# Scores of the segmented attention on 64 partitions a head, with the rotary exchange done by transfers inside the chip

## The chip, the cores and the metric

The kernel runs on one core of one Trainium2 chip. Its engines are TensorE (PE, with its weight loads shown apart as PEld), VectorE (DVE), ScalarE (ACT), GpSimd (POOL) and SyncE (SP, which here issues nearly all DMAs). The metric is the device time of one execution in microseconds (us). All arithmetic on the matrices is in float32.

## What is computed

Sixteen sequences of 256 tokens with 256 features pass through two layers, each adding to the residual x: a cross attention and a causal attention of 16 heads of 16 features; a feed-forward block with blockwise 4-bit rounding; a diffusion step followed by a segmented attention; and a mixture of eight experts. The change lies in the segmented attention, of 16 heads with 64 features. Cut to its core, the reference says:

```python
def _rotate_half(t):
    t2 = t.reshape(*t.shape[:-1], t.shape[-1] // 2, 2)
    return jnp.stack((-t2[..., 1], t2[..., 0]), axis=-1).reshape(t.shape)
x = seq * jax.lax.rsqrt(jnp.mean(seq * seq, axis=-1, keepdims=True) + eps) * g_norm
q, k, v = jnp.split(x @ W_qkv, 3, axis=-1)
q = q * cos + _rotate_half(q) * sin
k = k * cos + _rotate_half(k) * sin
...
k = jnp.concatenate((pmk, k), axis=-2)
v = jnp.concatenate((pmv, v), axis=-2)
scores = jnp.einsum('bhid,bhjd->bhij', q, k) * dh ** (-0.5)
scores = jnp.where(mask, scores, NEG_INF)
attn = jax.nn.softmax(scores, axis=-1)
out = jnp.einsum('bhij,bhjd->bhid', attn, v)
```

Segments have 128 tokens, so a sequence has two; each segment sees 16 learnt keys and values (pm) ahead of its own. The rotation pairs an even with an odd feature: the new even one is even x cos - odd x sin, the new odd one is odd x cos + even x sin.

## The kernel before

The program has two parts. `woven` (L292) runs everything up to the second residual, and `mixture` (L1034) the experts. Only the first is touched.

In `woven` nine generators, the stages, each yield one operation at a time: `stage_a` and `stage_e` the first two attentions, `stage_gate`, `stage_up` and `stage_down` the rounding of the feed-forward weights at the start, `stage_f` the feed-forward block, `stage_p` the diffusion and the projections of the segmented attention, `stage_g` its scores, `stage_v` its values. `weave` (L182) is a planner: it knows a cost for each operation (`Unit.cost`, L164), 4.5 us for the landing of a DMA issued by SP (`LANDING`) and 0.15 us for a hop between engines; it keeps for each tile when it was last written and read, takes the operation of all stages that could start first, issues it and goes on. So the order of each engine's queue is fixed when the program is built, and each engine executes it in that order. In the profile all woven operations have the same line, L160, where `Unit` makes the call; they are told apart by tiles.

The segmented attention works on groups of four heads; a sequence has four groups, the whole run 64. For each group, `project4` (L897) loads four pieces of weights (wq in two parts, wv, wo), multiplies them with the normalised input zT, and rotates query and key. The weights of a group are laid out by the host so that the 128 rows of the first half of the product are the 32 even features of four heads and those of the second half the 32 odd ones:

```python
yield g.pool.tensor_tensor(dst[0], by_seg(t1[:, 0, :]), by_seg(t2[:, 1, :]), ALU.subtract)
yield g.pool.tensor_tensor(dst[1], by_seg(t1[:, 1, :]), by_seg(t2[:, 0, :]), ALU.add)
```

Even and odd features of a head thus stand on the same partitions, one behind the other in the free dimension; t1 and t2 (f_t in the profile) are DVE's products with cosine and sine, read from PSUM, and POOL adds them into f_q or into `keys[n]`. `keys[n]` holds, for each half and segment, the 16 learnt keys ahead of 128 keys of the sequence.

`scores4` (L955) takes two heads at a time. For each segment it multiplies the even and then the odd features of each head, both on 32 partitions, and adds them up in PSUM: 2 segments x 2 halves x 2 heads = 8 matmuls of 32 partitions x 144 columns. DVE adds the causal mask and takes the maximum, ACT exponentiates, POOL scales. `values4` (L988) transposes the probabilities and multiplies by values and output weights. A group is admitted to `project4` when the values of the group three before it have been planned.

PSUM is held in two pairs of banks and four single banks, which stages take and give back. SBUF buffers are rings by name: t1 and t2 have one each, wq and wv two, f_q and wo three. `stage_p` begins when the first batch of the first attention and the three weight roundings are planned. `project_heads` (L467) does the rotation of the first attention with two products in b_t1 and b_t2 and a sum on POOL. `fetch_a` (L413) loads the inputs of a batch, xT with two buffers. In `stage_f` each batch also issues two DMAs of 1 MB that fill ysort with zeros.

Of the kernel before, what the change touches and what calls it, by code (L numbers as in the profile page):

```python
# [19 lines left out]
P = 128  # L20
# [42 lines left out]
def setup(ctx, tc, a, n_batch):  # L63
# [29 lines left out]
    nc.gpsimd.memset(k.zero, 0.0)  # L93

# [87 lines left out]
def weave(streams):  # L182
# [8 lines left out]
    def ready(op, engine):  # L191
# [4 lines left out]
        for x in op.outs:  # L196
            n = x.tensor.name
            before = [written.get(n), read.get(n)]
            ring = rings.get(getattr(x.tensor, "tag", None), [])
            if n not in ring and ring:  # L200
                bufs = x.tensor.bufs or x.tensor.tag_meta.bufs
                if len(ring) >= bufs:
                    before += [written.get(ring[-bufs]), read.get(ring[-bufs])]
            for p in before:
                if p:
                    t = max(t, p[0] + (HOP if p[1] != engine else 0.0))
# [85 lines left out]
def woven(k):  # L292
    nc, tc = k.nc, k.tc
    with ExitStack() as ctx:
# [13 lines left out]
        g.x, g.io, g.done = {}, {}, {"W": 0, "A": 0, "M": 0, "E": 0, "F": 0, "P": 0, "G": 0, "V": 0, "L": 0}  # L308
        with tc.manual_schedule():
            weave([stage_a(g), stage_e(g), stage_gate(g), stage_up(g), stage_down(g), stage_f(g), stage_p(g), stage_g(g), stage_v(g)])  # L310
# [102 lines left out]
def fetch_a(g, b):  # L413
# [3 lines left out]
    xT = g.a_.tile([P, 2, S], F32, name="xT", tag="xT", bufs=2)  # L417
# [49 lines left out]
def project_heads(g, hT):  # L467
# [8 lines left out]
    for st in range(2):  # L476
# [320 lines left out]

def stage_p(g):
    k, a = g.k, g.a
    yield lambda: g.done["A"] > 0 and g.done["W"] == 3  # L800
# [38 lines left out]
    g.keys = []  # L839
    for n in range(4):  # L840
        pmk = tile_l(g, [P, 2, 4 * PM], "pmk", 2)
        yield g.sp.dma_start(out=pmk, in_=a["pmk"][:, n])
        t = g.w.tile([P, 2, 2, PM + P], F32, name=f"keys{n}")
        for j in range(4):
            rows = row32(j, 32)
            src = pmk[rows, :, j * PM : (j + 1) * PM]
            yield g.pool.tensor_copy(t[rows, :, :, 0:PM], src.unsqueeze(2).to_broadcast([32, 2, 2, PM]))
        g.keys.append(t)
    g.mhalf = g.w.tile([P, 2], F32, name="mhalf")
# [47 lines left out]
def project4(g, n, zT):  # L897

    a = g.a
# [8 lines left out]
    by_seg = lambda t: t.rearrange("p (s t) -> p s t", s=2)  # L908
    for which in range(2):
# [4 lines left out]
        t1, t2 = tile_l(g, [P, 2, S], "f_t1"), tile_l(g, [P, 2, S], "f_t2")  # L914
# [13 lines left out]
    g.singles.append(one)  # L928
    return q, v, wo
# [25 lines left out]
def scores4(g, n, q, v, wo):  # L955
# [554 lines left out]
```

## Time and profile before

| what | value |
|---|---|
| median of 3 runs | 2941.87 us (2941.02 to 2943.33) |
| profiled execution, its own time | 2943.53 us |
| its span in the profile | 2941.8 us |
| mean granted TensorE clock | 0.963 |
| PE, PEld busy in the span | 2768.7, 2072.5 us |
| DVE, ACT, POOL busy | 1428.6, 924.0, 842.2 us |
| DMA moved | 265.66 MB, mean 90 GB/s |
| woven part | up to about 1897 us |

A group of the profile gives line, engine, operation, the tiles written and read, the shape and the count, then busy time in us and mean duration in ns, then the engine's idle time just before these instructions and what ended it. Records of PE overlap, so the busy time of a group divided by its count is its pace and is shorter than the mean duration of one. For a matmul the shape is given as rows x columns of the array used, then partitions x streamed columns. A row of the waits gives the waiting engine and tile, what ended the wait, the total in us, how often, and the longest. A stretch gives its length, then the busy us of PE, PEld, DVE, ACT and POOL with their instruction counts, the granted clock, the share of the DMA engines and GB/s.

### The profile page before, as it was taken

The numbers are of one execution on the slowest core, as the hardware profiler recorded it, in microseconds if no ns is written. First come the engines' busy times: TensorE is split into PE (matmuls) and PEld (weight loads), VectorE is DVE, ScalarE is ACT, GpSimd is POOL, SyncE is SP. The second block draws the span as 40 slices with busy tenths as digits, with TensorE's granted clock in tenths as the row PEclk, the third lists the DMA queues.
The fourth block names the chain that finished last, engine by engine and source line by source line (L and its number), as shares of the span: only waits on it lengthen the run. The fifth ranks groups of instructions, "written<-read, shape, count | busy, mean of one in ns | idle before, by whom it ended". The sixth has DMA issues, their size and how long they took to land. (4 is left out here: it accounts for less than half of the span.)

```text
span 2941.8 us, 42036 instructions
## 1 busy us (share of the span) xinstructions
PE 2768.7 (94%) x15979; PEld 2072.5 (70%) x15979; DVE 1428.6 (49%) x3073; ACT 924.0 (31%) x2416; POOL 842.2 (29%) x1023
## 2 busy tenths in 40 slices
PE   5899999999999999999999989689999999999999
PEld 3666667777777777767777767545566888888865
DVE  6566666676676676675776655413240000000023
ACT  2223333333333333423334333223321222222221
POOL 4333333433344343343343333202220000000034
PEclk7799999999899999999999999889999999999999
DMA  3122122122122132222221222231111355555523
GB/s 107 55 93 73 53 92 84 56 80 74 59 91 69 58 97 69 63 92 69 64 92 35 76 90 74 87 93 51 51 38 67 108 179 179 179 181 179 177 85 95
DMA packets 191230, 265.66 MB, mean 90 GB/s; under 512 B 34217, under 2 KB 161970, under 8 KB 181682
## 3 DMA queue, kind: packets, MB, share of 16 engines
q1 hardware_dynamic: 184882, 246.16, 26.2%
q0 software_dynamic: 6144, 16.79, 1.8%
q8 instruction: 128, 2.10, 0.3%
q14 instruction: 76, 0.62, 0.1%
HBM read 202.34 MB, written 60.56 MB: 89 GB/s over the span
## 5 line engine op out<-in xcount | busy, mean ns | idle before, releaser
L160 ACT ACTIVATE f_prob<-pair,f_stat 128x144 f32<-128x144 f32 x512 | 190.7, 377 | 270.2 <-DVE f_stat L160 258.8
L160 DVE TENSOR_TENSOR pair<-pair,mask 128x256 f32<-128x256 f32 (+1 forms) x384 | 197.8, 516 | 123.1 <-PE pair L160 83.2
L49 PE MATMUL bank<-ysT,w 128*128 128x256 f32 x1120 | 249.3, 381 | 5.7 <-ACT ysT L113 5.7
L160 PE MATMUL single<-e_zT,wq 128*128 128x256 f32 x1024 | 254.1, 392 | 0.0
L1155 POOL DMA_INDIRECT got<-osort,pos_o x64 | 62.3, 973 | 662.8 <-ACT hT L1103 608.5
L49 PE MATMUL bank<-w,ehT 128*128 128x256 f32 x1120 | 247.4, 379 | 0.0
L49 PEld LDWEIGHTS bank<-ysT,w 128*128 128x128 f32 x1120 | 211.3, 190 | 38.0 <-ACT ysT L113 9.9
L49 PEld LDWEIGHTS bank<-w,ehT 128*128 128x128 f32 x1120 | 212.8, 190 | 28.9
L160 PEld LDWEIGHTS single<-e_zT,wq 128*128 128x128 f32 x1024 | 193.4, 196 | 32.9 <-issue 2.7
L1140 ACT ACTIVATE ehT<-bank,own_b 128x256 f32<-128x256 f32 x280 | 132.5, 473 | 241.6 <-PE bank L49 241.6
L160 POOL TENSOR_SCALAR_AFFINE_SELECT b_e<-b_e 128x512 f32<-128x512 f32 x128 | 86.5, 676 | 329.9 <-ACT b_e L160 329.9
L160 PE MATMUL pair<-keys,f_q 32*128 32x144 f32 x2048 | 164.9, 300 | 0.9 <-ACT b_e L160 0.7
L160 PEld LDWEIGHTS pair<-keys,f_q 32*128 32x128 f32 x2048 | 137.2, 190 | 35.9 <-issue 28.6
L160 ACT ACTIVATE b_e<-pair 128x768 f32<-128x768 f32 x128 | 103.6, 810 | 166.4 <-PE pair L160 153.3
L160 PE MATMUL single<-wo,f_oT 128*128 128x256 f32 x512 | 129.8, 386 | 9.5 <-ACT f_oT L160 8.4
L160 POOL TENSOR_TENSOR f_q<-f_t,f_t 128x256 f32<-128x256 f32 x128 | 91.6, 734 | 160.9 <-DVE f_t L160 151.4
L160 PE MATMUL pair<-b_qkT 16*128 16x128 f32 (+1 forms) x1024 | 127.3, 373 | 11.0 <-ACT b_qkT L160 8.0
L1145 DVE COPY eo<-bank 128x512 f32<-128x512 f32 x35 | 24.2, 692 | 230.9 <-PE bank L49 230.9
L160 DVE TENSOR_REDUCE qpad<-pair 128x2 f32<-128x256 f32 (+1 forms) x256 | 131.0, 554 | 4.4
L1259 POOL DMA_INDIRECT ysort<-r_y,r_posi x64 | 62.6, 978 | 241.0 <-DMA ysort<-r_y,r_posi 97.0
L160 DVE TENSOR_TENSOR x<-x,single 128x512 f32<-128x512 f32 (+1 forms) x112 | 68.0, 607 | 128.7 <-PE single L160 128.1
L160 POOL TENSOR_TENSOR keys<-f_t,f_t 128x256 f32<-128x256 f32 x128 | 95.2, 762 | 118.8 <-DVE f_t L160 117.6
(295 smaller groups left out, 5319.7 us busy)
## 6 DMA issues: line engine op xcount, KB each, us to landing
w<-in_w SPq DMA_DIRECT2D x70, 1024.0 KB
ysort<-zero SPq DMA_DIRECT2D x32, 1024.0 KB
wq<-in_w_qk SPq DMA_DIRECT2D x128, 256.0 KB
wv<-in_w_v SPq DMA_DIRECT2D x64, 256.0 KB
wo<-in_w_out SPq DMA_DIRECT2D x64, 256.0 KB
ys<-ysort SPq DMA_DIRECT2D x35, 256.0 KB
osort<-eo SPq DMA_DIRECT2D x35, 256.0 KB
xT<-in_xT SPq DMA_DIRECT2D x16, 256.0 KB
```

Of the source, the lines that this page charges most:

```text
L49: nc.tensor.matmul(out, lhsT, rhs, start=start and i == 0, stop=stop and i == last)
L160: return Op([(self.name, self.cost(fn, outs, aps), lambda: call(*args, **kw))], outs, aps)
L1140: nc.scalar.activation(hT[:, f, :], ph, AF.Gelu_apprx_tanh, bias=b1[:, f : f + 1])
L1145: nc.vector.tensor_copy(o, po)
L1155: nc.gpsimd.indirect_dma_start(out=g, out_offset=None, in_=k.osort[:, :], in_offset=bass.IndirectOffsetOnAxis(ap=r.pos_o[:, i, t : t + 1], ...
L1259: nc.gpsimd.indirect_dma_start(out=k.ysort[:, :], out_offset=bass.IndirectOffsetOnAxis(ap=posi[:, i, t : t + 1], axis=0), in_=y, in_offset ...
```

## The change

The host's layout of weights and learnt keys stays. At the start of the program a new stage, `stage_order`, reads the query and key weights, reorders them on POOL so that a head's 32 even and 32 odd features are neighbours, and writes them to a scratch tensor `wqk` in DRAM, from which `project4` now loads; `stage_p` waits until this stage has been planned. The product then has a head's even features on 32 partitions and its odd ones on the next 32. The sine product has to be moved between these partitions, which four DMAs inside SBUF do, 32 partitions each, into a new tile t3; the signs go into the sine tables. One sum on POOL of twice the size replaces two, and the sum of the query is yielded after the key's transfers, that of the key after the values' projection. A score is one matmul on 64 partitions, with no accumulation. t1 and t3 have two buffers, t2 one. To make room, xT has one buffer and the first attention rotates in place in b_qk. The learnt keys are loaded by eight DMAs into the new layout. In the planner, a DMA of SP is no longer held back by an earlier DMA of SP on the same tile.

```diff
-                if p:
+                if p and not p[1] == engine == "SP":
...
-    xT = g.a_.tile([P, 2, S], F32, name="xT", tag="xT", bufs=2)
+    xT = g.a_.tile([P, 2, S], F32, name="xT", tag="xT")
...
-        t1, t2 = tile_a(g, 2 * D, "b_t1"), tile_a(g, 2 * D, "b_t2")
+        t2 = tile_a(g, 2 * D, "b_t2")
         for r in range(2):
-            yield g.dve.tensor_tensor(pairs(t1)[:, :, :, r], pairs(qk)[:, :, :, r], table(g.cos0), ALU.mult)
             sin = table(g.sin0 if r else g.nsin0)
             yield g.dve.tensor_tensor(pairs(t2)[:, :, :, r], pairs(qk)[:, :, :, 1 - r], sin, ALU.mult)
+        for r in range(2):
+            yield g.dve.tensor_tensor(pairs(qk)[:, :, :, r], pairs(qk)[:, :, :, r], table(g.cos0), ALU.mult)
         for i, dst in enumerate((qp, kp)):
             half = slice(i * D, (i + 1) * D)
-            yield g.pool.tensor_tensor(dst[:, st, :, 0:DH0], by_head(t1[:, half]), by_head(t2[:, half]), ALU.add)
+            yield g.pool.tensor_tensor(dst[:, st, :, 0:DH0], by_head(qk[:, half]), by_head(t2[:, half]), ALU.add)
...
+def stage_order(g):
+
+    k = g.k
+    for i in range(8):
+        cols = slice(i * 2 * P, (i + 1) * 2 * P)
+        raw, out = tile_l(g, [P, 2, S], "f_t1", 2), tile_l(g, [P, 2, S], "f_t3", 2)
+        yield g.sp.dma_start(out=raw, in_=g.a["w_qk1"][:, :, cols])
+        for c in range(2):
+            dst = out[:, c].rearrange("p (j r d) -> p j r d", j=4, r=2)
+            yield g.pool.tensor_copy(dst, raw[:, c].rearrange("p (r j d) -> p j r d", r=2, j=4))
+        yield g.sp.dma_start(out=k.wqk[:, :, cols], in_=out)
+    g.done["O"] = 1
...
-    yield lambda: g.done["A"] > 0 and g.done["W"] == 3
+    yield lambda: g.done["A"] > 0 and g.done["W"] == 3 and g.done["O"]
...
+    for rows in (row32(1, 32), row32(3, 32)):
+        for t in (g.sin1, g.sinq):
+            yield g.pool.tensor_scalar(t[rows], t[rows], -1.0, None, ALU.mult)
...
-        yield g.sp.dma_start(out=wq[:, which], in_=a["w_qk1"][:, :, cols])
+        yield g.sp.dma_start(out=wq[:, which], in_=k.wqk[:, :, cols])
...
-        t1, t2 = tile_l(g, [P, 2, S], "f_t1"), tile_l(g, [P, 2, S], "f_t2")
+        t1, t2, t3 = (tile_l(g, [P, 2, S], f"f_t{i}", 1 if i == 2 else 2) for i in (1, 2, 3))
...
-        dst = [g.keys[n][:, r, :, PM:] if which else by_seg(q[:, r, :]) for r in range(2)]
-        yield g.pool.tensor_tensor(dst[0], by_seg(t1[:, 0, :]), by_seg(t2[:, 1, :]), ALU.subtract)
-        yield g.pool.tensor_tensor(dst[1], by_seg(t1[:, 1, :]), by_seg(t2[:, 0, :]), ALU.add)
+
+        for i in range(4):
+            yield g.sp.dma_start(out=t3[row32(i, 32)], in_=t2[row32(i ^ 1, 32)])
+        dst = g.keys[n][:, :, :, PM:] if which else q.rearrange("p c (s t) -> p c s t", s=2)
+        yield from join
+        join = iter([g.pool.tensor_tensor(dst, by_seg(t1), by_seg(t3), ALU.add)])
...
     g.singles.append(one)
+    yield from join
     return q, v, wo
...
         for st in range(2):
-            for r in range(2):
-                for i in range(2):
-                    rows = row32(j0 + i, 32)
-                    lhsT, rhs = q[rows, r, st * P : (st + 1) * P], keys[rows, r, st, :]
-                    yield g.pe.matmul(sc[i][:, st, :], lhsT, rhs, start=r == 0, stop=r == 1)
+            for i in range(2):
+                rows, c = row32(2 * i, 64), j0 // 2
+                lhsT, rhs = q[rows, c, st * P : (st + 1) * P], keys[rows, c, st, :]
+                yield g.pe.matmul(sc[i][:, st, :], lhsT, rhs, start=True, stop=True)
```

More of the change, by code (lines that the diff above doesn't have):

```diff
@@ L93, in setup @@
     nc.gpsimd.memset(k.zero, 0.0)
+    k.wqk = dram.tile([P, 2, 2 * H * DH1], F32, name="wqk")
     k.xd = [dram.tile([S, D], F32, name=f"xd{b}") for b in range(n_batch)]
@@ L307, in woven @@
         g.live, g.kT = {}, {}
-        g.x, g.io, g.done = {}, {}, {"W": 0, "A": 0, "M": 0, "E": 0, "F": 0, "P": 0, "G": 0, "V": 0, "L": 0}
+        g.x, g.io, g.done = {}, {}, {"W": 0, "O": 0, "A": 0, "M": 0, "E": 0, "F": 0, "P": 0, "G": 0, "V": 0, "L": 0}
         with tc.manual_schedule():
-            weave([stage_a(g), stage_e(g), stage_gate(g), stage_up(g), stage_down(g), stage_f(g), stage_p(g), stage_g(g), stage_v(g)])
+            weave([stage_a(g), stage_e(g), stage_gate(g), stage_up(g), stage_down(g), stage_order(g), stage_f(g), stage_p(g), stage_g(g), stage_v(g)])
 def load(g, pool, name, shape, src):
@@ L839, in stage_p @@
     g.keys = []
+    pmk = tile_l(g, [P, 4, 2, PM], "pmk")
+    for j in range(4):
+        for r in range(2):
+            src = a["pmk"][row32(j, 32), :, r, j * PM : (j + 1) * PM]
+            yield g.sp.dma_start(out=pmk[row32(2 * (j % 2) + r, 32), :, j // 2, :], in_=src)
     for n in range(4):
-        pmk = tile_l(g, [P, 2, 4 * PM], "pmk", 2)
-        yield g.sp.dma_start(out=pmk, in_=a["pmk"][:, n])
         t = g.w.tile([P, 2, 2, PM + P], F32, name=f"keys{n}")
[L844 to L847, printed above, removed]
+        yield g.pool.tensor_copy(t[:, :, :, 0:PM], pmk[:, n].unsqueeze(2).to_broadcast([P, 2, 2, PM]))
         g.keys.append(t)
+    for rows in (row32(1, 32), row32(3, 32)):
+        for t in (g.sin1, g.sinq):
+            yield g.pool.tensor_scalar(t[rows], t[rows], -1.0, None, ALU.mult)
     g.mhalf = g.w.tile([P, 2], F32, name="mhalf")
@@ L897, in project4 @@
 def project4(g, n, zT):
-    a = g.a
+    k, a = g.k, g.a
     wq = tile_l(g, [P, 2, 2, 2 * P], "wq", 2)
@@ L907, in project4 @@
     q = tile_l(g, [P, 2, S], "f_q", 3)
-    by_seg = lambda t: t.rearrange("p (s t) -> p s t", s=2)
+    by_seg = lambda t: t.rearrange("p c (s t) -> p c s t", s=2)
+    join = ()
     for which in range(2):
```

## The prediction

> **What bounds the kernel now.** I read the busy shares of the engines and the 40 slices first, then the stretches of 200 us, then the waits of TensorE, then the single score blocks in the timeline. The page's first two parts:
>
> ```profile
> PE 2768.7 (94%) x15979; PEld 2072.5 (70%) x15979; DVE 1428.6 (49%) x3073; ACT 924.0 (31%) x2416; POOL 842.2 (29%) x1023
> ...
> PE   5899999999999999999999989689999999999999
> ...
> DVE  6566666676676676675776655413240000000023
> ```
>
> The woven stages (attention, feed-forward, segmented attention, all batches at once) fill slices 1 to 25, up to 1897 us; the mixture fills the rest and is not touched. One stretch of the woven part (length, then busy us of PE, PEld, DVE, ACT, POOL):
>
> ```profile
> 1000.00:1200.00 200.00, 192.27 (x1339) 146.86 (x1338) 138.22 (x283) 72.65 (x224) 74.87 (x88) 0.99 0.26 82
> ```
>
> PE works 96% of it, DVE 69%, POOL 37%, the DMA engines 26%. From 200 to 1600 us PE idles about 8 us in 200. So PE's work sets the time here. From 1660 to 1900 us the early stages have run out and PE idles 28.7 of 240 us. What PE waits for between 120 and 1900 us is short:
>
> ```profile
> PE single L160 <- POOL d_h L160: 18.3, 13, 2.5
> PE single L160 <- POOL f_prob L160: 17.5, 9, 5.1
> PE single L160 <- POOL c_y L160: 11.0, 9, 3.7
> ```
>
> No wait on the rotary work or on a DMA of the segmented attention is among the long ones. The groups that the change touches:
>
> ```profile
> L160 PE MATMUL pair<-keys,f_q 32*128 32x144 f32 x2048 | 164.9, 300 | 0.9 <-ACT b_e L160 0.7
> L160 PEld LDWEIGHTS pair<-keys,f_q 32*128 32x128 f32 x2048 | 137.2, 190 | 35.9 <-issue 28.6
> ...
> L160 POOL TENSOR_TENSOR f_q<-f_t,f_t 128x256 f32<-128x256 f32 x128 | 91.6, 734 | 160.9 <-DVE f_t L160 151.4
> ...
> L160 POOL TENSOR_TENSOR keys<-f_t,f_t 128x256 f32<-128x256 f32 x128 | 95.2, 762 | 118.8 <-DVE f_t L160 117.6
> ```
>
> A matmul of the program is two records. A score block (a pair of heads, 8 matmuls) is 16 records; there are 128 blocks. The timeline gives a block its price from its start to the next operation's start:
>
> ```profile
> 1021.35 1.09 PE L160 MATMUL single<-ident,f_prob 128*128 128x128 f32 x8
> 1022.39 1.25 PE L160 MATMUL pair<-keys,f_q 32*128 32x144 f32 x16
> 1023.57 1.99 PE L160 MATMUL single<-wv,e_zT 128*128 128x256 f32 x8
> ```
>
> The block costs 1023.57 - 1022.39 = 1.18 us, 74 ns a record. Eight full-array records of 128 columns cost 1.04 us, 130 ns each; of 256 columns (1018.67 to 1020.49 us in the same view) 228 ns each. A lone record of 144 columns would by that line cost about 130 + 98 x 16/128 = 142 ns. So the two heads' 32-row matmuls run beside each other, 1.9 to 1.
>
> **What the Trainium skill says.** "TensorEngine Tiling (Array Packing)", Theoretical Speedup and Key Properties: a contraction of at most 64 rows allows up to 2 times by packing, and tiles at other rows work independently. The 1.9 agrees for two tiles of 32 rows; no row of this trace has two tiles of 64 rows. "TensorE: Matmul & The Clock Gate", LDWEIGHTS: a load takes its time from the columns, not from the rows. The trace agrees: medians are 187, 185 and 190 ns for 16, 32 and 128 rows at 128 columns. "DMA: Bandwidth & Descriptors", Anatomy of one DMA: a DMA's wait is made by the issuing sequencer before dispatch, so what stands behind it on SP stands too. The trace agrees: SP's queue waited 1344 us for PE in 73 places, and holds later loads meanwhile.
>
> **The change, part by part.**
>
> *Scores.* A block becomes 4 matmuls of 64 rows, 8 records, still alternating between two row groups. Unknown is their pace. Lower bound: the weight loads' pace in a block, 1.03/16 = 64 ns; upper: no overlap, 142 ns. I take today's 74 ns, because columns, loads and alternation stay. A block then costs 8 x 0.074 = 0.59 us, and 128 blocks give back 128 x 0.59 = 75 us of PE (82 at 64 ns; at 142 ns only 128 x 0.04 = 5).
>
> How much of it reaches the end? 28 of 128 blocks lie after 1660 us. Where PE is 96% busy I take 90% of 100 x 0.59, i.e. 53 us: the other engines keep their rates and DVE has 30% to spare. After 1660 us, where PE already waits (17.5 us there for f_prob from POOL), 60% of 16.5, i.e. 10 us. Sum 63 us.
>
> *Rotary on DVE and POOL.* DVE's four products a group stay. POOL's four 128x256 additions become two of 128x512; that shape costs 1267 ns (x<-x,bout), against 734 or 762 twice: 64 x (2 x 0.734 + 2 x 0.762 - 2 x 1.267) = 29 us less of POOL. It is worth nothing by itself.
>
> *The exchange.* Eight transfers a group, 512 in all, 64 KB each: 33.5 MB in some 1700 us, 20 GB/s beside today's 77 (800 to 1000 us: 75). One exchange: SP takes 0.33 to 0.38 us an issue (pmk, also 64 KB), four make 1.4 us; a pmk issued at 116.77 had landed by 118.74, about 2.0 us; the 512 KB pmv issued at 97.43 was used at 102.85, 5.4 us, the upper bound for a loaded queue. So 3.3 us from product to sum, up to 7. Three queues are passed. (1) On DVE the key's sine product must wait for the query's exchange, its buffer being single. In the changed program's order of instructions a median 3.7 us of DVE work lies between the two (at today's durations), some 5.3 us of time at 70% busy: mostly covered. A sixth have 2.4 us or less; there mask additions and maxima of the scores queue behind. (2) On POOL the sums stand until the data land; behind them are the masks of the first attention (b_e) and the scaling of f_prob. The order puts the query's sum after the key's transfers are issued. (3) On SP the next group's wq, wv and wo queue behind eight transfers: 8 x 0.35 = 2.8 us of issue. A group comes every 27 us, so normally free; bursts of groups (1458.8 and 1474.1 us) feel it. The path from the key's projection to the scores has at least 4.4 us of PE work between them in the new order, over 14 in 54 of 64 groups: covered, and if not, some 2.5 us. I take 6 us for all of this; bounds 0 and 64 x 1 = 64 us.
>
> *Start.* The new stage reorders the weights once: 8 loads and 8 stores of 256 KB, 16 POOL copies of 128x256. No such copy is in the trace; nearest are 0.23 (32x64) and 0.86 us (cosq, 128x256): 4 to 14 us of POOL, which is 45% busy in the first 60 us. There PE idles 30 of 60 us, so a delay passes on. The projections begin only at 187 us, so their new gate costs nothing; what can be late is the weight quantisation and the first heads, behind copies that wait for loads. I take 5 us, bounds 0 and 15.
>
> *Edits at nothing.* The in-place rotation of the first attention: before, the second half's first cosine product already waited for POOL's additions; now its bias addition and value copy too, 0.69 + 0.41 us. Other PE work hides it; uncovered 16 x 1.1 = 18 us. A single xT: its load goes out after the last use; uncovered 2 us a batch. Eight small pmk loads and fewer key copies, before 187 us: nothing, at most 3 us. The planner's rule on SP only reorders.
>
> Sum: -63 + 6 + 5 = -52 us. The profiled execution took 2943.5 us (span 2941.8, 1.7 around it); minus 52 is 2891. The median, 2941.9, lies 1.6 below, so I say 2890.
>
> **Rivals.**
> (a) *The saving passes almost whole*: 82 us at the load pace, starts and exchanges free: 2862 to 2866. For it: PE is 96% busy. Against: the tail's waits. Chance 0.08.
> (b) *Transfers take the saving's place*: DVE or POOL stand 0.5 us or more at each of 128 exchanges, 40 us passing on to PE: 2890 + 36 = 2926, from 2915 to 2938. For it: DMAs behind the 1 MB zero fills of ysort land late (the wq issues after one at 1408.62 took 3.67 us instead of 1.2), and masks queue behind. Against: the slack above. Chance 0.13.
> (c) *Slower*: two 64-row tiles do not run beside each other. The place is the score block: 8 x 142 = 1.14 us instead of 1.18, and the 11 us of start and exchange remain, with masks later: 2942 - 5 + 11 = 2948, up to 2960. It decides from about 126 ns a record, where 128 x (1.18 - 1.01) = 22 us, half realised, just pays the 11. For it: the single 64-row tile (d_hT) costs 22.3/64 = 348 ns a record against about 266 for its 128-row neighbours. Against: that is one tile amid others of another size, and 32-row tiles do overlap. Chance 0.12. That the change doesn't do what it says is this case.
>
> **Numbers.** My forecast has 0.67, from 2866 to 2915. What a measurement of this kernel can tell from no change is 0.2%, 6 us. Faster 0.84: forecast, (a) and nearly all of (b). Slower 0.12: (c) and the far end of (b). Same 0.04. The range 2862 to 2936 leaves out (c) and the end of (b).
>
> **What would show it.** Right: 1024 score records, a block of 0.55 to 0.65 us, PE busy down by 70 to 80 us, woven stages ending about 1845 us, mixture unchanged. Wrong: a block over 0.9 us; POOL or DVE waiting long for DMA of f_t; more idle of PE before pair<-keys,f_q; SP holding wq so that PE waits for a DMA; the projections starting after 195 us.

## The result, and the profile after

| what | before | after |
|---|---|---|
| median | 2941.49 us (2941.02 to 2943.33) | 2973.31 us (2967.28 to 2977.13) |
| profiled execution, its span | 2943.53, 2941.8 us | 2977.13, 2975.4 us |
| busy PE, DVE, ACT, POOL | 2768.7, 1428.6, 924.0, 842.2 us | 2737.1, 1410.8, 943.6, 831.4 us |
| DMA moved | 265.66 MB | 303.18 MB |

The changed kernel is slower by 1.1%: ratio 1.0109, 95% interval 1.0081 to 1.0137. From here on, the bracket behind a time gives the lowest and highest run; a ratio is to the kernel before, run beside each experiment, and its bracket is the 95% interval. TensorE does less work and the program takes longer. The page after, engines, slices and the groups of the rotary part:

```profile
PE 2737.1 (92%) x14955; PEld 2016.8 (68%) x14955; DVE 1410.8 (47%) x3027; ACT 943.6 (32%) x2462; POOL 831.4 (28%) x903
...
PE   5899999999998999999999887679999999999999
...
L161 PE MATMUL single<-e_zT,wq 128*128 128x256 f32 x1024 | 254.5, 393 | 24.8 <-DMA wq<-wqk 23.7
...
L161 POOL TENSOR_TENSOR f_q<-f_t,f_t 128x512 f32<-128x512 f32 x64 | 81.3, 1270 | 253.8 <-DMA f_t<-f_t 197.1
```

Slices 23 to 27 (about 1640 to 2010 us after) have gone from 9, 8, 9, 6, 8 to 8, 8, 7, 6, 7: the hole is at the end of the woven part. Three waits are new: TensorE for the weights wq, POOL's sums for the transfers, and VectorE's sine product for them:

```profile
DVE f_t L161 <- DMA f_t<-f_t: 33.3, 27, 3.0
```

All woven operations now have line L161. The score group, from the groups with shapes kept apart:

```profile
L161 PE MATMUL pair<-keys,f_q 64*128 64x144 f32 x1024 | 100.2, 315 | 6.3 <-DVE vpad L161 5.2 <-POOL keys L161 1.0
```

It was 164.9 us and is 100.2: 64.7 us less. The timeline shows that two 64-row tiles do run beside each other:

```profile
1007.93 0.76 PE L161 MATMUL pair<-keys,f_q 64*128 64x144 f32 x8
...
1008.62 0.66 PE L161 MATMUL single<-ident,a_e 128*128 128x128 f32 x4
```

A block takes 1008.62 - 1007.93 = 0.69 us, 86 ns a record, against 1.18 us. But all of PE's busy time fell only by 2768.7 - 2737.1 = 31.6 us; where the other 33 us went is taken up in the last section. A stretch in the middle (same columns as before) has gone from 192 to 187 us of PE:

```profile
1000.00:1200.00 200.00, 186.99 (x1171) 138.54 (x1172) 131.05 (x266) 73.89 (x217) 74.85 (x76) 0.97 0.30 87
```

To see where the time lies I took marks from the timeline of TensorE: the start of the first projection onto wq; the starts of the diffusion of sequences 0 and 13 (records x,lap); and the end of the last values (single<-wo,f_oT). They are rounded to whole us. The expectations below count sequence 13 as batch 14.

| | first wq | sequence 0 | sequence 13 | last values | 13 to the end |
|---|---|---|---|---|---|
| before | 187 | 174 | 1669 | 1896 | 227 |
| after | 196 | 183 | 1667 | 1929 | 262 |

The start is 9 us later, the middle has regained 11 of the hoped-for 50, and the end is 35 us longer. The mixture behind it is unchanged (1046 us).

### The profile page after: what moved, and what is told of

It reads as the page before. It is cut to its first block, busy times and chain, and to the rows that moved or that the text cites. A ratio compares the mean times of both kernels' runs of the same rounds, so it can differ in the third digit from the quotient of the medians.

```text
span 2975.4 us, 40964 instructions
## 1 busy us (share of the span) xinstructions
PE 2737.1 (92%) x14955; PEld 2016.8 (68%) x14955; DVE 1410.8 (47%) x3027; ACT 943.6 (32%) x2462; POOL 831.4 (28%) x903
## 2 busy tenths in 40 slices
DMA packets 220734, 303.18 MB, mean 102 GB/s; under 512 B 43753, under 2 KB 175090, under 8 KB 211186
## 5 line engine op out<-in xcount | busy, mean ns | idle before, releaser
L161 PE MATMUL single<-e_zT,wq 128*128 128x256 f32 x1024 | 254.5, 393 | 24.8 <-DMA wq<-wqk 23.7
L161 ACT ACTIVATE f_prob<-pair,f_stat 128x144 f32<-128x144 f32 x512 | 190.9, 377 | 226.8 <-DVE f_stat L161 218.3
L161 DVE TENSOR_TENSOR pair<-pair,mask 128x256 f32<-128x256 f32 (+1 forms) x384 | 197.7, 515 | 124.7 <-PE pair L161 78.9
L161 PEld LDWEIGHTS single<-e_zT,wq 128*128 128x128 f32 x1024 | 192.4, 196 | 57.5 <-issue 27.6
L161 POOL TENSOR_SCALAR_AFFINE_SELECT b_e<-b_e 128x512 f32<-128x512 f32 x128 | 90.3, 705 | 293.9 <-ACT b_e L161 286.1
L161 POOL TENSOR_TENSOR f_q<-f_t,f_t 128x512 f32<-128x512 f32 x64 | 81.3, 1270 | 253.8 <-DMA f_t<-f_t 197.1
L161 ACT ACTIVATE b_e<-pair 128x768 f32<-128x768 f32 x128 | 103.5, 808 | 149.1 <-PE pair L161 130.7
L161 PE MATMUL single<-wo,f_oT 128*128 128x256 f32 x512 | 136.0, 400 | 11.4 <-ACT f_oT L161 9.7
L161 PE MATMUL pair<-b_qkT 16*128 16x128 f32 (+1 forms) x1024 | 130.3, 376 | 7.4 <-DVE qpad L161 3.8
L1169 DVE COPY eo<-bank 128x512 f32<-128x512 f32 x35 | 24.2, 691 | 230.9 <-PE bank L49 230.9
L161 DVE TENSOR_REDUCE qpad<-pair 128x2 f32<-128x256 f32 (+1 forms) x256 | 131.0, 554 | 4.4
L161 PE MATMUL single<-wv,e_zT 128*128 128x256 f32 x512 | 131.1, 402 | 0.0
L161 PE MATMUL pair<-b_qS,b_qkT 17*128 17x256 f32 (+1 forms) x1024 | 122.8, 360 | 6.6 <-ACT b_qS L161 3.7
L161 DVE TENSOR_TENSOR x<-x,single 128x512 f32<-128x512 f32 (+1 forms) x112 | 68.0, 607 | 124.6 <-PE single L161 124.4
L161 PEld LDWEIGHTS pair<-b_qS,b_qkT 17*128 17x128 f32 x1024 | 96.9, 197 | 40.8 <-issue 16.3
```

Source lines behind the costliest of these rows:

```text
L161: return Op([(self.name, self.cost(fn, outs, aps), lambda: call(*args, **kw))], outs, aps)
L1169: nc.vector.tensor_copy(o, po)
```

## The experiments

My first theory was that the exchange stands in the queues of SP, DVE and POOL. The second was that the planner misjudges the new score matmul: its rule knows packing for 32 rows only and puts 0.29 us on a 64-row matmul that takes 0.69/4 = 0.17 us, so that every queue is ordered for work that isn't there. The rival to both is that any new order scatters the time. Only x1 and x2 keep the changed kernel's order; every other experiment is planned anew.

### The same order, without the transfers and with doubled scores

x1_no_exchange keeps the plan, and leaves out only the 512 transfers; the sine product goes straight to t3:

```diff
-        yield g.dve.tensor_tensor(t2, pq, sin.unsqueeze(1).to_broadcast([P, 2, S]), ALU.mult)
+        planned = g.dve.tensor_tensor(t2, pq, sin.unsqueeze(1).to_broadcast([P, 2, S]), ALU.mult)
+        made = g.dve.tensor_tensor(t3, pq, sin.unsqueeze(1).to_broadcast([P, 2, S]), ALU.mult)
+        yield with_call(planned, made.choices[0][2])
...
-            yield g.sp.dma_start(out=t3[row32(i, 32)], in_=t2[row32(i ^ 1, 32)])
+            yield with_call(g.sp.dma_start(out=t3[row32(i, 32)], in_=t2[row32(i ^ 1, 32)]), lambda: None)
```

> Leaves out the rotary exchange: the sine product is written straight to the tile that POOL adds, so even and odd features are not swapped; the order planned for every engine is kept, without the 512 transfers. Theory exchange (the transfers, their issue on SP and the waits for them hold DVE, POOL and the next weights): about 2890 us, woven stages ending near 1850, no wait of PE for wq after 1700 us. Rival order (the new plan and the other edits cost the time, not the transfers): 2955 us or more, the slow tail stays.

Measured: 2934.04 us (2931.96 to 2935.86), ratio 0.9972 (0.9953 to 0.9990), between the two expectations. With no queue reordered, the transfers, with the waits for them, cost 2973.3 - 2934.0 = 39 us. The marks give sequence 0 to 13 in 1464 us instead of 1484, and 245 us to the end instead of 262. But without transfers the kernel is only 8 us below the kernel before: in this order most of the saved TensorE time is missing as well.

x2_doubled keeps the plan and makes each score matmul twice:

```diff
-                yield g.pe.matmul(sc[i][:, st, :], lhsT, rhs, start=True, stop=True)
+                op = g.pe.matmul(sc[i][:, st, :], lhsT, rhs, start=True, stop=True)
+                twice = lambda call=op.choices[0][2]: [call() for _ in range(2)]
+                yield with_call(op, twice)
```

> Every score matmul is executed twice into the same place, in the order of the changed kernel: 8 matmuls of 64 rows a block, so PE's work is as before the change again. If PE still sets the time: 128 x 0.5 = 64 us more, about 3035 us. If PE no longer sets it, the added work falls into idle time: 2975 to 3000 us.

Measured: 2991.41 us (2988.81 to 2996.45), ratio 1.0167 (1.0144 to 1.0190), the second case. Its score group:

```profile
L161 PE MATMUL pair<-keys,f_q 64*128 64x144 f32 x2048 | 176.6, 306 | 3.8 <-DVE vpad L161 3.8
```

176.6 - 100.2 = 76 us of TensorE work were added and the time grew by 18 us: in this order an added microsecond of score work costs about 0.24 us, not the 0.84 of my sum (63 of 75). This is the net price, for two things came back: TensorE's idle time (span less busy time) fell from 238.3 to 202.3 us, and its other records took 27 us less together, in good part because they ran for less time at half clock (151 instead of 199 us).

### Other queue, other layout

x3_act_queue issues the four transfers on ScalarE's queue, at a planned cost of 0.6 us each:

```diff
+    return Op([("ACT", 0.6, lambda: call(out=dst, in_=src), LANDING)], [dst], [src])
...
-            yield g.sp.dma_start(out=t3[row32(i, 32)], in_=t2[row32(i ^ 1, 32)])
+            yield on_act(g, t3[row32(i, 32)], t2[row32(i ^ 1, 32)])
```

> The exchange's transfers are issued by ACT's queue instead of SP's; the planner counts 0.6 us of ACT for each. Theory exchange, through SP (weights parked behind the transfers): the waits for wq after 1700 us go, 25 to 35 us less, about 2943 us, less what ACT's 300 us of issues cost. Theory exchange, through the landing alone: no change or slower, 2965 to 2990 us.

Measured: 3975.76 us (3973.55 to 3980.37), ratio 1.3506, neither case. It doesn't test what I meant it to: the planner's new exemption names SP only, so here each of the four transfers was planned behind the landing of the one before it on the same tile. As the issuing queue was changed too, it isn't a clean price of the diff's line on SP either, and it tells nothing on SP's queue.

x4_host_order lets the host lay out the weights in the new order and drops `stage_order`:

```diff
-    qk = w[:, : 2 * n].reshape(D, 2, 4, 4, DH1 // 2, 2).transpose(0, 1, 2, 5, 3, 4).reshape(D, 2 * n)
+    qk = w[:, : 2 * n].reshape(D, 2, 4, 4, DH1 // 2, 2).transpose(0, 1, 2, 3, 5, 4).reshape(D, 2 * n)
```

> The weights come from the host in the new order, so the stage that reorders them is gone. If the late start (first projection at 196 instead of 187 us) is passed on to the end: 2964 us. If it is absorbed: 2970 to 2976 us. Theory order allows any change by 10 us either way, since the plan is made anew.

Measured: 2973.68 us (2968.49 to 2977.15), ratio 1.0100 (1.0076 to 1.0124), no change. The first projection came at 189 us instead of 196, and nothing of it is left in the total: TensorE's wait for wq in the end was 24.2 us as before.

### The planner's costs

y1_plan_pe halves the planned cost of a 64-row matmul, in one line of `Unit.cost` (which also takes in a few other matmuls of 64 rows, mainly the 64 records onto d_hT):

```diff
-            side = (2 if rows <= 32 else 1) * (3 if cols <= 32 else 2 if cols <= 64 else 1)
+            side = (2 if rows <= 64 else 1) * (3 if cols <= 32 else 2 if cols <= 64 else 1)
```

> Only the planner's cost of a score matmul of 64 rows is changed, to half (0.149 instead of 0.288 us), nearer to the 0.17 us that the trace shows; each engine does the same work in another order. Theory plan (the order made with wrong costs keeps the score's saving from being used): 2935 to 2955 us, against 2973 of the changed kernel. Theory exchange alone: 2965 to 2980 us.

Measured: 2939.44 us (2932.73 to 2946.89), ratio 0.9989 (0.9982 to 0.9996): 34 us less than the changed kernel, the second theory's success so far. Sequence 0 to 13 took 1447 us, the end 264.

y2_plan_sp plans 0.6 us for an issue on SP instead of 0.06:

```diff
         if self.name == "SP":
-            return 0.06
+            return 0.6
```

> Only the planner's cost of issuing a DMA on SP is changed, from 0.06 to 0.6 us, which the trace shows (588 ns for a transfer of the exchange). Theory plan: the order places the sums and the next weights later, DVE and POOL stand less for the transfers, 2945 to 2960 us. Theory exchange alone (the chain of issues itself is what is late): 2965 to 2985 us.

Measured: 2967.22 us (2961.94 to 2970.51), ratio 1.0085 (1.0068 to 1.0101), 6 us less, as the exchange alone would have it.

y3_side_edits is the kernel before with the planner's line on SP, a single xT and the rotation in place, as in the change:

```diff
-                if p:
+                if p and not p[1] == engine == "SP":
...
-    xT = g.a_.tile([P, 2, S], F32, name="xT", tag="xT", bufs=2)
+    xT = g.a_.tile([P, 2, S], F32, name="xT", tag="xT")
...
-            yield g.dve.tensor_tensor(pairs(t1)[:, :, :, r], pairs(qk)[:, :, :, r], table(g.cos0), ALU.mult)
...
+            yield g.dve.tensor_tensor(pairs(qk)[:, :, :, r], pairs(qk)[:, :, :, r], table(g.cos0), ALU.mult)
```

> The kernel before with the side edits alone: one xT buffer, the first attention's rotation in place, the planner's rule for two DMAs of SP. If they are free, as predicted: 2935 to 2950 us. If they are what eats the score's saving: 2965 us or more.

Measured: 2943.76 us (2940.71 to 2949.03), ratio 1.0004 (0.9995 to 1.0013). Together these edits cost nothing.

y4_no_exchange_replanned leaves out the transfers before the plan is made, and yields the sums at once:

```diff
-        t1, t2, t3 = (tile_l(g, [P, 2, S], f"f_t{i}", 1 if i == 2 else 2) for i in (1, 2, 3))
+        t1, t2 = (tile_l(g, [P, 2, S], f"f_t{i}", 2) for i in (1, 3))
...
-        for i in range(4):
-            yield g.sp.dma_start(out=t3[row32(i, 32)], in_=t2[row32(i ^ 1, 32)])
...
-        yield from join
-        join = iter([g.pool.tensor_tensor(dst, by_seg(t1), by_seg(t3), ALU.add)])
+        yield from iter([g.pool.tensor_tensor(dst, by_seg(t1), by_seg(t2), ALU.add)])
```

> Leaves out the rotary exchange, as the first experiment did, but the plan is made without it too, each sum directly behind its products. Theory plan: the order made for transfers of 4.5 us cost the first experiment its gain, so this one comes to 2885 to 2905 us. Rival (side edits or engines other than PE limit): 2925 to 2940 us, as the first experiment.

Measured: 2918.63 us (2917.74 to 2919.35), ratio 0.9917 (0.9900 to 0.9933), between the two cases. z1_no_exchange_plan_pe has both, this edit and y1's line:

> The changed kernel with both corrections at once: the planner's cost of a 64-row score matmul is halved, and the exchange is left out, so the sine product of the other features isn't moved and the rotation is computed with unmoved products (this part of the computation is left out). Theory (two causes that add up: an order made for score matmuls of 0.29 us that take 0.17, worth 34 us by itself, and the exchange, worth 55 us by itself when the order is made without it): between 2880 and 2895 us, the saving of 63 us of TensorE reaching the end nearly whole. Rival, that the two overlap because both only loosen one chain in the last batches: 2910 to 2920, no better than the exchange left out alone (2918.6). Rival, that every new order moves the time by some ten us either way: anything from 2900 to 2940.

Measured: 2890.91 us (2883.44 to 2898.25), ratio 0.9819 (0.9785 to 0.9853), as the theory of two causes had it. The exchange is now priced three times: 39 us (after against x1), 55 us (after against y4), 49 us (y1 against z1). Only the first leaves the order as it was; the two others hold a new order as well.

z3_before_wrong_cost overrates the scores in the kernel before by as much:

```diff
-            side = (2 if rows <= 32 else 1) * (3 if cols <= 32 else 2 if cols <= 64 else 1)
+            side = ((1.44 if n == PM + P else 2) if rows <= 32 else 1) * (3 if cols <= 32 else 2 if cols <= 64 else 1)
```

> The kernel before, with nothing changed but the planner's cost of its own score matmuls, raised from 0.15 to 0.20 us, so that a block is overrated by the same 0.45 us as in the changed kernel; the instructions are the same, only their order differs. Theory (the order made with a cost that is too high loses what the score matmuls save): 2965 to 2980 us, as the change loses 34 us by it. Rival, that the overrated cost does harm only together with the transfers, by spreading the groups against SP's queue: 2940 to 2948, no change.

Measured: 2968.12 us (2963.43 to 2972.93), ratio 1.0094 (1.0061 to 1.0127), 24 us slower than the kernel before beside it. Again for the second theory.

### The weights ahead of the transfers, and a second sine buffer

z2_weights_first loads wq and wv of the next group just ahead of this group's transfers (`weights` is the part of `project4` that loads them, now on its own; it also runs once ahead of the first group):

```diff
+        if not which and g.done["P"] + 1 < 4 * g.B:
+            yield from weights(g, (n + 1) % 4)
         for i in range(4):
             yield g.sp.dma_start(out=t3[row32(i, 32)], in_=t2[row32(i ^ 1, 32)])
```

> The changed kernel with the halved cost of a 64-row score matmul, and with the wq and wv of the next group issued by SP ahead of this group's eight transfers instead of behind them; wo stays. Theory (in the last batches TensorE waits for weights whose issue stands behind transfers that wait for DVE): the wait of TensorE for wq, 22.9 us in eight places with the halved cost alone, is gone, the stretch after batch 14's start falls from 264 us to 235 to 245, and the time from 2939 to between 2910 and 2922 us. Rival, that the chain is product, transfer, sum, scores and the weights only stand in its shadow: the wait moves to scores waiting for the sums on POOL, 2930 to 2940. Rival, that the transfers share the DMA engines with the weights and slow them: no change, 2939.

Measured: 2965.01 us (2963.50 to 2978.18), ratio 1.0089 (1.0058 to 1.0119). A miss: the wait for wq is gone and the end is 251 us instead of 264, but sequence 0 to 13 took 1486 us instead of 1447. The next four runs ask why.

u1_two_t2 gives the key's sine product a buffer of its own (with the halved cost, as all of these):

```diff
-        t1, t2, t3 = (tile_l(g, [P, 2, S], f"f_t{i}", 1 if i == 2 else 2) for i in (1, 2, 3))
+        t1, t3 = tile_l(g, [P, 2, S], "f_t1", 2), tile_l(g, [P, 2, S], "f_t3", 2)
+        t2 = tile_l(g, [P, 2, S], "f_t2", 1, "e_lx" if which else "f_t2")
```

> The changed kernel with the halved cost of a 64-row score matmul, and the sine product of the key in a buffer of its own (that of e_lx, idle then), so that VectorE's product for the key doesn't wait for the query's transfers. Theory (part of the exchange's cost is VectorE standing for the transfers, 32.8 us in 26 places, with the first attention's products queued behind it): that wait is gone and the time falls from 2939 to between 2920 and 2932 us. Rival, that the path is SP's eight issues of 0.59 us before the next weights: 2935 to 2942. Rival, that transfers start earlier and so delay the weights more: slower, 2945 to 2955.

Measured: 2931.49 us (2928.61 to 2943.85), ratio 0.9955 (0.9938 to 0.9971), 8 us less than y1. VectorE's wait for transfers is gone, but POOL's sums now wait 327 us for them (207 for f_q, 120 for keys) instead of 166, and another order was planned: sequence 0 to 13 took 1486 us, 39 more than in y1, and the end 228, 36 less.

u2_two_t2_weights_first has both edits, u1's and z2's:

> The same own buffer, together with wq and wv of the next group issued ahead of this group's transfers (which alone gave 2965 us). Theory (the earlier weights hurt because they put the query's transfers off by 2 us, and VectorE and then the first attention's head sums on POOL stand behind them): the middle falls back from 113 to 108 us a batch or less, the wait for wq stays away, 2910 to 2930 us. Rival, that POOL's sum, which stands for the landing ahead of the head sums, is the one that passes it on: the middle stays at 112 to 114 us, 2955 to 2970.

Measured: 2937.95 us (2924.50 to 2951.72), ratio 0.9985 (0.9969 to 1.0001). Between the two cases: 27 us below z2, yet sequence 0 to 13 took 1501 us, no less than with the single buffer; the end took 217.

u3_weights_first_at_end has the earlier weights from group 53 on only:

```diff
+    if not g.next:
+        yield from weights(g, n)
...
+        if not which and 53 <= g.done["P"] < 4 * g.B - 1:
+            yield from weights(g, (n + 1) % 4)
```

> Halved cost of a 64-row score matmul, and wq and wv of the next group issued ahead of the transfers only from group 53 on (the last two batches and a half); the single sine buffer stays. Theory: the middle keeps 108 us a batch, the stretch after batch 14's start goes from 264 to about 252 us as with earlier weights everywhere, 2924 to 2932 us. Rival, that what the end gains is only what the middle lost (the end starts with less queued): no change, 2936 to 2942.

Measured: 2929.43 us (2926.15 to 2933.49), ratio 0.9953 (0.9937 to 0.9970), as the theory had it: sequence 0 to 13 in 1451 us, the end 255 instead of 264, TensorE's wait for wq 1.1 us instead of 22.9. With 0.5% less than the kernel before, this version beats both; the next part shows how little a half per cent proves here.

u4_both_costs has both planned costs, y1's line and y2's:

> The changed kernel with two costs of the planner corrected: that of a 64-row score matmul halved, and that of an issue on SP 0.6 us instead of 0.06. If the order doesn't cover the exchange because the planner takes eight issues for 0.5 us instead of 4.7: 2915 to 2930 us. If the coupling is in the program (buffers, queues in order) and no order covers it, or the planner's landing time of 4.5 us covers the issue already: 2930 to 2945, the 6 us that this cost gave alone at most.

Measured: 2990.81 us (2987.67 to 3003.19), ratio 1.0168 (1.0139 to 1.0197). Neither case. Against y2 (2967.22), the corrected score cost made it 24 us slower.

### A neutral constant

That left the rival, so three more runs change only what a change of stage costs TensorE in the plan, which is meant to scramble the order without favouring anything:

```diff
-TURN = 0.1
+TURN = 0.12
```

> The kernel before with the planner's constant for a change of stage on TensorE at 0.12 us instead of 0.10, so another order of the same instructions. Theory (the score cost matters by itself): within 10 us of the kernel before, 2934 to 2954. Rival (any new order scatters by 20 us or more): outside of that, to either side.

> The changed kernel with the same neutral constant at 0.12 us. Theory: within 10 us of the changed kernel, 2963 to 2983, so slower than the kernel before again. Rival: outside of that, and then the changed kernel's 1.1% are in part the luck of one order.

> The changed kernel with the halved cost of a 64-row score matmul and the neutral constant at 0.12 us. Theory: 20 to 45 us below the changed kernel with that constant, 2930 to 2950. Rival: no more below it than the scatter that the two other runs show, or above it.

Measured: the kernel before 2959.14 us (2950.97 to 2960.50; ratio 1.0051, 1.0035 to 1.0068), the changed kernel 2988.32 (2987.04 to 2990.92; 1.0149, 1.0132 to 1.0166), the changed kernel with halved cost 3007.91 (2998.49 to 3017.83; 1.0227, 1.0208 to 1.0245). All three lie outside the range of their theory (the kernel before is taken from the runs beside v1; beside the changed kernel it took 2941):

| median in us, by the constant | 0.10 | 0.12 | difference |
|---|---|---|---|
| kernel before | 2944 | 2959 | 15 |
| changed kernel | 2973 | 2988 | 15 |
| changed kernel, halved cost | 2939 | 3008 | 68 |

So an order that means nothing moved two of the versions by 15 us and the third by 68. All three moved up; with one other value tried, it isn't shown that the constant is neutral. The corrected score cost now costs 20 us. Its five tests stand at -34 (after to y1) and -28 (y4 to z1), which speak for the second theory, as do the 24 us that the wrong cost added to the kernel before (z3); +24 (y2 to u4) and +20 (v2 to v3) speak against it. The second theory is not shown; that order scatters the time by tens of us is. What sets a good order apart stays open.

The change itself is slower by 32 us with one constant and by 29 with the other. But the same instructions with the halved cost are level with the kernel before at 0.10 and 49 us slower than it at 0.12, so the sign of the change's effect belongs to the order too. What no new order blurs is the 39 us that the exchange costs in the changed kernel's order.

The wait for wq came back in the two new orders of the changed kernel, in more places and twice as long: 47.1 us in 15 places with the halved cost, and without it:

```profile
PE single L161 <- DMA wq<-wqk: 45.6, 10, 7.1
```

## Where the exchange takes its time

*In the middle it goes through VectorE and POOL.* After and x1 have the same order on each engine, so their waits from 400 to 1500 us may be set side by side. After:

```profile
PE single L161 <- POOL qpad L161: 12.0, 5, 3.3
...
PE single L161 <- POOL c_y L161: 6.4, 5, 1.7
```

x1:

```profile
PE single L161 <- POOL qpad L161: 1.0, 5, 0.2
PE single L161 <- POOL c_y L161: 0.9, 1, 0.9
```

The transfers add 11.0 + 5.5 = 16.5 us here to what TensorE waits for the heads of the first attention (qpad) and the rounding of the feed-forward input (c_y), of the 20 us between the marks. One of the five places of qpad, in the timeline after (start, length, engine, operation, and in brackets the idle time ahead of it and what ended it):

```profile
1164.45 0.41 SPq L161 DMA_DIRECT2D x<-in_x  x1
...
1165.00 8.74 SPq L161 DMA_DIRECT2D f_t<-f_t  x8
...
1167.46 0.68 DVE L161 TENSOR_TENSOR f_t<-single,cos 128x512 f32<-128x512 f32 x1
...
1170.57 0.69 DVE L161 TENSOR_TENSOR f_t<-single,sin 128x512 f32<-128x512 f32 x1 [2.42 <-DMA f_t<-f_t]
...
1173.89 0.68 DVE L161 TENSOR_TENSOR b_qk<-pair,bqkv 128x512 f32<-128x512 f32 x1
...
1177.22 0.33 PE L161 MATMUL single<-ident,qpad 128*128 128x128 f32 x1 [2.73 <-POOL qpad L161]
```

SP is still loading the next sequence's inputs when the query's sine product is ready (its record goes from 1161.82 to 1162.50), so the transfers are issued only from 1165.00 on. The key's sine product needs the single t2 and stands until 1170.57. Behind it on VectorE wait two masks and then b_qk, whose sum on POOL TensorE needs. The same place in x1:

```profile
1154.60 0.68 DVE L161 TENSOR_TENSOR f_t<-single,cos 128x512 f32<-128x512 f32 x1
...
1155.20 0.68 DVE L161 TENSOR_TENSOR f_t<-single,sin 128x512 f32<-128x512 f32 x1
...
1158.51 0.68 DVE L161 TENSOR_TENSOR b_qk<-pair,bqkv 128x512 f32<-128x512 f32 x1
...
1161.84 0.33 PE L161 MATMUL single<-ident,qpad 128*128 128x128 f32 x1 [0.21 <-POOL qpad L161]
```

From the sine product to b_qk it is 3.3 us in both; the 2.5 us more between the two products are what arrives at TensorE. The c_y goes through POOL's queue, as one of its five places shows, after:

```profile
913.71 1.27 POOL L161 TENSOR_TENSOR keys<-f_t,f_t 128x512 f32<-128x512 f32 x1 [3.60 <-DMA f_t<-f_t]
...
915.06 0.35 DVE L161 RECIPROCAL q_inv<-q_unit 128x32 f32<-128x32 f32 x1
...
917.16 1.06 POOL L161 TENSOR_TENSOR q_xn<-c_y,q_inv 128x512 f32<-128x512 f32 x1
...
922.13 0.66 PE L161 MATMUL single<-ident,c_y 128*128 128x128 f32 x4 [1.68 <-POOL c_y L161]
```

and in x1:

```profile
903.80 0.35 DVE L161 RECIPROCAL q_inv<-q_unit 128x32 f32<-128x32 f32 x1
904.24 1.06 POOL L161 TENSOR_TENSOR q_xn<-c_y,q_inv 128x512 f32<-128x512 f32 x1 [0.50 <-DVE q_inv L161]
```

The key's sum stands 3.6 us for its transfers; f_pm, f_prob (not shown) and q_xn, the first step towards c_y's rounding, are behind it. In x1 q_xn starts 0.1 us after q_inv has ended, here 1.75 us, and TensorE waits 1.68. The other places I have not followed.

z2, in an order of its own, agrees with the path through VectorE: its transfers are issued behind the weights (1.8 us), and from 400 to 1500 us TensorE waited 15.9 us in nine places for POOL's qpad, a wait that isn't in y1's list. u2 doesn't: it has no such wait of VectorE and is no faster in the middle. So these paths are shown for the changed kernel's order, and not as the only ones.

*At the end it goes through SP.* The timeline after, in sequence 14:

```profile
1796.25 7.10 SPq L161 DMA_DIRECT2D f_t<-f_t  x8
...
1803.45 1.23 SPq L161 DMA_DIRECT2D wq<-wqk  x2
...
1806.65 3.37 PE L161 MATMUL single<-e_zT,wq 128*128 128x256 f32 x8 [6.66 <-DMA wq<-wqk]
...
1811.13 1.89 PE L161 MATMUL single<-e_zT,wq 128*128 128x256 f32 x8
```

The weights for the next group are issued behind eight transfers, the last four of which wait for VectorE. TensorE's queue has this projection next, and it stands for 6.7 us; then the same eight records take 3.37 us instead of 1.89. The two pieces of wq landed 3.1 us after their issues began, and by the semaphores' records of all 128 the median from issue to landing is 3.15 us after, 4.42 in x1 and 4.56 before. So the transfers' bytes don't slow the weights; it is the late issue. u3 removes this wait (22.9 us in y1, 1.1 in u3), but its end is only 9 us shorter than y1's. It doesn't become as short as before (227): the first of TensorE's waits there are now others.

```profile
PE single L161 <- POOL f_prob L161: 22.8, 10, 4.5
...
PE pair L161 <- POOL keys L161: 10.2, 6, 3.3
```

## Why the prediction was wrong, point by point

*Score block: right, a term a little small.* 86 ns a record instead of 74, within the bounds of 64 and 142; 64.7 us of the group instead of 75. (The 82 us at 64 ns, on which rival (a) rests, should have been 128 x (1.18 - 0.51) = 86, and (a) then ends at 2856, not 2862.) Rival (c), no overlap, is out, although the sign it stood for came true.

*Realised share: wrong, the step "Where PE is 96% busy I take 90%".* I took 90% in the dense middle, because PE was 96% busy and the others kept their rates, and 60% at the end: 63 us. In the changed kernel's order all of the change but the transfers gave 8 us (x1), and doubling the scores in that order says 24%: if the first microseconds taken away are worth as much as those added, 0.24 x 64.7 = 15 us. In another order, also without the transfers, 53 us came out (z1). So the share isn't set by the busy time: in a fixed order TensorE waits in short places for the others, and what it saves can turn into waiting and into a lower clock, as x2 shows in reverse. Why one order yields 8 and the other 53 stays open.

*Exchange: wrong, the step "I take 6 us for all of this".* It costs 39 us in its own order. My bound of 64 held it, and rival (b), with its 40 us, had the size and two of the places (VectorE and POOL; SP it didn't name), but I gave it 0.13, and its range ended at 2938, since it kept the rest of the saving. The single terms: an issue takes 0.59 us instead of 0.35, as the trace after has it (shortest, middle and longest in ns, first and last start):

```profile
L161 SPq DMA_DIRECT2D f_t<-f_t x512: 507/588/1818, 203.0 to 1903.3; - x171
...
L161 SPq DMA_DIRECT2D pmk<-in_pmk x8: 589/597/1776, 117.6 to 123.3; - x8
```

I took pmk as the nearest row for its 64 KB. But it lay on 128 partitions, where a transfer has 32 (the second row shows the changed kernel's pmk, 8 KB on 32 partitions, at 0.60); two of its four issues took 0.42 and 0.43, not 0.38 at most; and the trace before also had wq's issues with a median of 0.61. The landing I had right: a transfer landed 2.0 us after its issue began (median; 6.2 the longest). A group's eight make 4.7 us of issue and stretch to 7.1 or 8.7 us with what they wait for. From the end of the query's sine product to the release of the key's it was 1170.57 - 1162.50 = 8.1 us in the place above, 2.5 of them for SP's loads of inputs; in the quieter place in sequence 14 it was 1800.19 - 1796.19 = 4.0. I had 3.3 and named 7 as the limit. So VectorE's median 3.7 us of work covered less than I thought: it stood 33.3 us in 27 places of 64, not in a sixth. Of what stands behind the waits I named masks, b_e and f_prob; what TensorE missed in the middle was qpad and c_y. That bursts of groups feel SP's queue was right, but I priced the burst at 2.8 us and left out that at the end little work is left that could hide it. Three of the signs of being wrong came true: POOL and VectorE waiting for f_t, SP holding wq, and projections after 195 us.

*Start: right.* The first projection came 9 us later, within 0 to 15, though x4, without the stage and in a new order, found nothing of it in the total.

*Edits at nothing: right*, as far as y3 goes, with 1.0004 (pmk's eight small loads weren't in it). But "The planner's rule on SP only reorders" was too light a reason for nothing: a reordering alone is worth 15 us or more.

*Sum.* Saving -15, exchange +39, start and edits 0: +24, where +32 were measured. The missing 8 are less than what a meaningless change of the order does (15 and more). x1's -8 for all but the transfers, start and order included, closes the sum, as it must. My range had no term for the order at all, which the diff had changed from beginning to end.

## What to carry to other kernels

Where a program fixes the order of all queues, price a saving on the busiest engine by what it frees in that order: double the operation in place and see what the end pays, before taking its busy time for the path. In the places followed here, a transfer inside the chip cost not by its bytes but by its places in the queues: the issue, what stands behind it on the issuing engine, the engine whose next product needs the same buffer, and the engine whose sum waits for the landing. And when a planner is involved, measure a few meaningless changes of its constants first (here 15, 15 and 68 us); differences below what they do are not evidence for a cause.

## What the runs showed of the hardware

TensorE's records can grow after a wait: 3.37 us instead of 1.89 for eight 256-column records after 6.7 us of idling. The Trainium skill, "TensorE: Matmul & The Clock Gate", What's actually happening, says that the clock is halved by default and released by sustained work; the trace agrees (busy time of TensorE, then the granted clock, in a stretch behind the wait and in a later one):

```profile
1806.60:1808.40 1.80, 1.75 (x4) 0.50 0.76 267
...
1811.13:1813.00 1.87, 1.87 (x12) 1.00 0.14 33
```

Short waits can do it too: two of 0.94 and 0.77 us between 812.80 and 816.20 us were followed by a stretch at half clock, in which eight 256-column records took 3.20 us.

```profile
812.80:816.20 3.40, 1.69 (x22) 1.00 0.08 19
816.20:819.60 3.40, 3.40 (x15) 0.50 0.27 60
```

From 1640 to 1880 us the mean granted clock is 0.90 after, where it was 0.95 before. So a wait can be paid in part twice, once as idling and once as slower records. This is a part of why TensorE's busy time fell by 31.6 us and not by 64.7. Counted from the records of both traces, those other than the scores ran 168 us at half clock before and 199 after, by estimate 15 us of lost time. Another 10 us were never there to save: score records lay over others for 25.7 us before and 15.5 after, and the group's busy time counts them in full. Some 8 us of the 33 stay open.

The other surprise is the issue of a small transfer between partitions, 0.59 us on SP: more than that of the 64 KB pieces of pmk on 128 partitions before (0.33 to 0.43), and as much as that of wq's 256 KB (0.61 before) or of the 8 KB pieces of pmk on 32 partitions after (0.60). The bytes don't decide it here; what does, I have not tested.
